# A four-layer graph network on one core: first matrix on two queues, the last mask turn one tile earlier, first weights and sigmoids around the end of a projection, one divisor product for the last tile

## The chip, the cores and the metric

The kernel runs on one core of a Trainium2 chip. The metric is the device time of one execution in microseconds, the median over several runs. The engines are named as in the profile: PE (matmul), DVE (vector), ACT (scalar), POOL (GpSimd) and SP (sync); PEld is PE's weight load, which overlaps its matmuls. SP, ACT and POOL can each issue DMAs.

## The reference, cut to what matters

A graph of 2708 nodes with 512 features passes four layers, each `x = layernorm(x + layer(x, adj))`. Layer 0 averages the first 64 neighbours of each node, layer 1 all of them, layer 2 is an eight-head graph attention, layer 3 an eight-head one followed by a one-head one and a two-layer MLP.

```python
# layer 0: mean of the first 64 neighbours, one matrix each for it and for x itself
keep = Ab & (jnp.cumsum(Ab.astype(jnp.int32), axis=1) <= neibor_num)
nb_mean = (keep @ X) / jnp.maximum(cnt, 1.0)
xj = leaky_relu(nb_mean @ W_nb.T + b_nb); xi = leaky_relu(X @ W_line.T + b_line)
# layer 1
agg = mask @ x / jnp.maximum(deg, 1.0)
out = relu(concat([x @ W_self + b_self, agg @ W_nb + b_nb]) @ W_comb + b_comb)
# layers 2 and 3, each head
Wh = einsum('ni,hio->hno', h, W)
e = leaky_relu(f1[:, :, None] + f2[:, None, :], 0.2)     # f1, f2 = Wh . a1, Wh . a2
attention = softmax(where(adj > 0, e, -9e15), axis=-1)
h_prime = einsum('hnm,hmo->hno', attention, Wh)
```

## The kernel before

The nodes are cut into NT = 22 tiles of 128 rows (the last, LAST, has 20). A scheduler orders each engine's instructions; where the kernel wants a fixed order it says so: `pe(...)` chains PE's instructions in program order, and `tc.issue_after(x)` holds what is issued inside it behind `x` on its engine. Each engine works through its own list in order.

**Layer 0, first loop (L291 to L339).** `transpose_weight` (L136) loads a 512x512 matrix in four pieces of 128 rows from SP, turns each on PE and copies it with DVE. Then, tile by tile: `keep_y` (product with the first matrix, split in a high part by ACT and a low one by DVE), the product with the second matrix, and beside them the adjacency: rows are loaded by POOL as bf16 (`load_mask`, L255), turned to 0/1 by an ACT sigmoid (`count`, L260), limited to the first 64 by DVE scans (`place`, L264), and turned on PE with ACT signs into `maskT` (`turn`, L273). 14 of the 22 row blocks are done there, at most one per tile; the loop at L320 turns a block one tile after it was placed. Its last pass, at the last tile, turns all. The remaining 8 row blocks are loaded from L353 on into `spare` and `w`; `spare` lies where the row blocks of the first loop were, so its first load waits for the last turn.

**Layer 0, second loop (L467).** PE multiplies `kT`, made from `maskT` by ACT (L350), with the high and low parts (L477), with the remaining row blocks' `count` (L262) between the `kT` of ACT.

**Projections (`project`, L587).** For each tile: transpose of the rows, product with all heads' weights into PSUM `pm` (L642), then `dcol` and `b` on DVE, `ecol` and `ucol` as exponentials on ACT (L663, L664), `vcol` (L677), `vrow` (L622, stored to DRAM by an ACT DMA), and `R2`, the scaled rows, on DVE (L671). The last tile stands twice in its key tile: on partitions 0 to 19 for even heads and 32 to 51 (from TWIN) for odd heads (L651 to L661, two halves `k`). After the last tile of a block of 11, DVE splits `ecol` and `ucol*ecol` into bf16 parts `parts_m`, `parts_c` (L680 to L689). The small copies of this split are L581 to L585.

**Attention (`heads_attention`, L755; `Weights`, L698).** 16 runs in all: two layers, each two blocks of columns (1408 and 1300) by four pairs of heads. In a run, for each of the 22 key tiles `j` (order L887: ten tiles, then LAST, then the rest) and each head: DVE makes the weights `e = max(v, u) * mask` (L718), ACT marks by a sigmoid where `v` is below `u` (`above`, L741, the tile `c`), and PE multiplies `e` with R2 into `po` (L910). For LAST there is one `e` and one `c` for both heads. `divisors` (L810) adds up, four key tiles at a time, the products of `c` with `parts_c`, for each head in four column groups (L814). Buffers: five `e`, eleven `c`; an `e` buffer is free when PE and ACT have read it. `vrow`'s PSUM comes free for `po` once ACT has read the last of it.

`Weights.first` (L730) lets a projection make four weight tiles ahead, from tile NT − 6 = 16 on, one per tile: `att.early` (two key tiles by two heads), held in order behind R2 of the tile before (L665). Their sigmoids are issued only in the attention (L907), where the scheduler is free to move them forward.

Of the kernel before, what the change touches and what calls it, by code (L numbers as in the profile page):

```python
# [13 lines left out]
AF = mybir.ActivationFunctionType  # L14
# [4 lines left out]
P = 128  # L19
D = 512  # L20
KD = D // P
EPS = 1e-5
ALPHA = 0.2
# [7 lines left out]
def kernel(  # L31
# [9 lines left out]
    nc = tc.nc  # L41
# [91 lines left out]
        nc.scalar.copy(dst[:, :, :n], ps[:, :, :n])  # L133
        return dst

    def transpose_weight(room, psum, dst, src):  # L136

        for ki in range(KD):
            wr = room[ki]
            nc.sync.dma_start(wr, src[ki * P:(ki + 1) * P, :])  # L140
            ps = psum.tile([P, KD, P], F32, name="ps_tr")
            for ko in range(KD):
                pe(nc.tensor.transpose(ps[:, ko, :], wr[:, ko * P:(ko + 1) * P], ident))
            nc.vector.tensor_copy(dst[:, :, ki * P:(ki + 1) * P], ps)
# [56 lines left out]
    with ExitStack() as phase:  # L201
# [89 lines left out]
        with ExitStack() as ph:  # L291
            st = ph.enter_context(tc.tile_pool(name="l0a", bufs=1))
            wnT, wlT = weight(), weight2
            room = [maskT[:, G + k, :4 * D].bitcast(F32) for k in range(2 * KD)]

            xs = rows_of(x)
            xTs = early(0, NT, lambda t, order=as_it_comes: transposed(ahead, ps_tr, xs(t), rows(t), "xT", order))

            transpose_weight(room[:KD], ps_tr, wnT, l0_w_nb)
            lows = {}
            for t in range(2):
                xT = xTs(t, order=pe)
                lows[t] = keep_y(t, P, product(xT, P, wnT, 0, pe))
            transpose_weight(room[KD:], ps_tr, wlT, l0_w_line)
            b_line = bias(bcast(l0_b_line, D))
            masks = early(1, HERE, lambda i: load_mask(i, st.tile([P, N], BF16, name="m", bufs=3)))
            masks(0)
            nc.gpsimd.memset(maskT[:, NT - 1, :], 0.0)  # L310
            nc.gpsimd.memset(maskT[:, :, N:], 0.0)
            counted = turned = 0
            for t in range(NT):
                n = rows(t)
                if t > 1:
                    lows[t] = keep_y(t, n, product(xTs(t, order=pe), n, wnT, 0, pe))
                xT = xTs(t)
                if t + 1 < NT:
                    xTs(t + 1, order=pe)
                while turned < counted - (t + 1 < NT):  # L320
                    for _ in turn(turned, masks(turned), lambda: sums(BF16, (P, G, P)), pe):
                        pass
                    turned += 1
                now = counted < min(HERE, -(-(t - 1) * HERE // (NT - 5)))
                if now:
                    m, places = masks(counted), st.tile([P, N // 2], BF16, name="places", bufs=1)
                    with tc.issue_after(highs[t].ins):
                        count(counted, m)
                    with tc.issue_after(lows[t].ins):
                        place(counted, m, places, 0, 2)  # L330
                pm = product(xT, n, wlT, 1, pe)
                u = sm.tile([P, D], F32, name="u")
                nc.vector.tensor_add(u[:n], pm[:n], b_line[:n])  # L333
                low = rows_made = leaky(u[:n], u[:n])
                nc.gpsimd.dma_start(r0_dram[t * P:t * P + n, :], u[:n])
                if now:
                    with tc.issue_after(low.ins):
                        place(counted, m, places, 1, 2)
                    counted += 1  # L339
# [238 lines left out]
    def split(pool, dst, src):  # L578

        rest = pool.tile([P, NT, H], F32, name="rest", bufs=1)[:, :src.shape[1], :src.shape[2]]  # L580
        nc.vector.tensor_copy(dst[:, :, :, 0], src)  # L581
        nc.vector.tensor_sub(rest, src, dst[:, :, :, 0])
        nc.vector.tensor_copy(dst[:, :, :, 1], rest)
        nc.vector.tensor_sub(rest, rest, dst[:, :, :, 1])
        nc.vector.tensor_copy(dst[:, :, :, 2], rest)  # L585

    def project(name, source, layer, v_dram, cuts, turned=None, first=None):  # L587
# [12 lines left out]
        with ExitStack() as ph:  # L600
# [16 lines left out]
            def keep_v(t):  # L617
                n = rows(t)
                vrow = sm.tile([heads, P], F32, name="vrow")
                ps = ps_v.tile([P, P], F32, name="ps_v")  # L620
                nc.tensor.transpose(ps[:heads, :n], bs[t][:n, :heads], ident[:n, :n])
                nc.scalar.activation(vrow[:, :n], ps[:heads, :n], AF.Exp, scale=ALPHA - 1.0)  # L622
                nc.scalar.dma_start(v_dram[:, t * P:t * P + n], vrow[:, :n])

            for t in range(NT):
# [55 lines left out]
                if t == z - 1:  # L681
                    if heads > 1:
                        ue = sm.tile([P, NT, H], F32, name="ue", bufs=1)[:, :z - a]
                        nc.vector.tensor_mul(ue, ucol[:, a:z], ecol[:, a:z])
                        split(sm, parts_m[:, a:z], ue)
                        for k in range(2):
                            nc.vector.tensor_scalar(pairs_c[:, a:z, :, k, 6 * k:6 * k + 3], parts_m[:, a:z, k::2, :],
                                                    -1.0, None, op0=OP.mult)
                            split(sm, pairs_c[:, a:z, :, k, 6 * k + 3:6 * k + 6], ecol[:, a:z, k::2])  # L689
            keep_v(NT - 1)  # L690
            sq = sm.tile([P, NT * H], F32, name="sq", bufs=1)[:, :NT * heads]
            dd = dcol[:, :, :heads]
# [5 lines left out]
    class Weights:  # L698


        def __init__(self, stack, name, blocks, v_dram):
            self.blocks, self.v_dram = blocks, v_dram
            self.W = max(self.width(b) for b in range(len(blocks)))
            self.pool = stack.enter_context(tc.tile_pool(name=f"{name}_att", bufs=2))

# [24 lines left out]
        def first(self, t):  # L730

            if t == NT - 8:
                self.vs = [self.load(0, h) for h in range(2)]
                self.early = []
            i = t - (NT - 6)
            if not 0 <= i < 4:
                return None
            self.early.append(self.weights(0, i % 2, i // 2, self.vs[i % 2]))
            return self.made
# [12 lines left out]
        oT_dram.append(dram.tile([D, (z - a) * P], F32, name=f"oT_dram{i}"))  # L752
        rc_dram.append(dram.tile([H, 12 * P], F32, name=f"rc_dram{i}"))

    def heads_attention(name, att, as_rows, meanwhile={}):  # L755

# [1 line left out]
        with ExitStack() as ph:  # L760
# [48 lines left out]

            def divisors(b, p, pair):  # L810
                for i, j, hs, cs in pair:
                    for h, c in zip(hs, cs):
                        for g, c0, c1 in groups(b):
                            pe(nc.tensor.matmul(p[32 * g:32 * g + 12, :c1 - c0], parts_c[:, j, h, :], c[:, c0:c1],  # L814
                                                start=(i == 0 and h == hs[0]), stop=(i == NT - 1 and h == hs[1])))
# [72 lines left out]
            for r, (b, h0) in enumerate(runs):  # L888
# [9 lines left out]
                for i_, j in enumerate(order):  # L898
                    if j == LAST:
                        es = [att.weights(b, h0, j, both)] * 2  # L900
                        cs = [att.above(b, h0, j, es[0])] * 2
                        if r + 1 < len(runs):
                            both = att.load_both(*runs[r + 1])
                    else:
                        es = ([att.weights(b, h, j, v) for h, v in zip(hs, vs)] if r or i_ > 1 else
                              att.early[2 * i_:2 * i_ + 2])
                        cs = [att.above(b, h, j, e) for h, e in zip(hs, es)]  # L907
                    for i, (c0, c1) in enumerate(parts):
                        for k, (h, e) in enumerate(zip(hs, es)):
                            pe(nc.tensor.matmul(po[i][HO * k:HO * k + HO, :c1 - c0], R2[:, j, h * HO:(h + 1) * HO],  # L910
                                                e[:, c0:c1], start=(i_ == 0), stop=(i_ == NT - 1)))
                    if len(pair) == 4:
                        divisors(b, pd[r % 2], pair)
                        pair = []
                    pair.append((i_, j, hs, cs))
                    for step in todo.get(i_, ()):
                        step()
# [206 lines left out]
    vd = [dram.tile([heads, N], F32, name=f"v_dram{i}") for i, heads in enumerate((H, H, 1))]  # L1124
    for i, source in enumerate((plain, summed)):
        with ExitStack() as ph:
            att = Weights(ph, f"a{2 + i}", blocks, vd[i])
            project(f"p{2 + i}", source, i, vd[i], blocks, first=att.first)
            heads_attention(f"a{2 + i}", att, i == 0, {
                9 + 4 * t: [lambda t=t: ready.update({t: elu_turned(None, t, t + 1)})] for t in range(3)} if i else {})  # L1130
    ph4 = fast.enter_context(ExitStack())
    att = Weights(ph4, "a4", quads, vd[2])
# [329 lines left out]
```

## Time and profile before

| | us |
|---|---|
| median of 3 runs | 2969.1 (2968.95 to 2974.76) |
| profiled execution | 2975.79 |
| its span | 2973.9 |
| PE / DVE / ACT busy in the span | 2879.2 / 1998.3 / 1536.7 |
| layer 0 first loop, second loop begins | 0 to 217.7 |
| projection of layer 2 / attention runs | about 880 to 975 / 975 to 1519 |
| projection of layer 3 / attention runs | about 1525 to 1626 / 1626 to 2173 |

"Busy" counts overlapping instructions of one engine once. A line of the timeline gives start, length, engine, line, operation, output and input, the number of instructions merged, and in brackets the idle time of that engine just before and what ended it. A busy PE is not a PE at its peak: its ends are modelled, and a stretched row of matmuls can hide short waits. Several groups run in parallel engines, so shares don't add up.

### The profile page before, as it was taken

To read this page: it belongs to the slowest core of one execution; us is meant where nothing else is said; L and a number is where in the kernel's file an instruction comes from. 1 tells how busy PE (TensorE), PEld (TensorE's weight loads), DVE (VectorE), ACT (ScalarE), POOL (GpSimd) and SP (SyncE) were. 2 spreads that over 40 slices of the span, in tenths; PEclk is the share of its full clock that TensorE was granted. 3 is DMA by queue.
4 is the path that set the end of the run, shared out by engine and by line. 5 is a ranking of instruction groups with operands and counts; after the bars stand their busy time and mean duration, and the time that the engine had idled before them with its cause. 6 is when DMAs were issued, how large, how long until landed. Compare 5 with 4: busy or idle time off the path is not lost. (4 is left out here: it accounts for less than half of the span.)

```text
span 2973.9 us, 36611 instructions
## 1 busy us (share of the span) xinstructions
PE 2879.2 (97%) x14462; PEld 1605.8 (54%) x14462; DVE 1998.3 (67%) x2406; ACT 1536.7 (52%) x1775; POOL 207.9 (7%) x344
## 2 busy tenths in 40 slices
PE   8999999999999999999999999999999999999998
PEld 3447766448888343444456334434475555555555
DVE  5966637543234899999977999999963535445342
ACT  3545533113224899999966899999951000000001
POOL 1110100101110000000012000000000000000001
PEclk9999999999999999999999999999999999999999
DMA  4532426322222011111144111121061000000000
GB/s 121 122 91 57 113 87 171 130 62 92 79 74 81 21 52 46 38 45 44 32 126 147 40 40 39 41 64 37 29 160 61 4 25 14 25 14 16 15 18 24
DMA packets 121153, 185.61 MB, mean 62 GB/s; under 512 B 41741, under 2 KB 66562, under 8 KB 120972
## 3 DMA queue, kind: packets, MB, share of 16 engines
q1 hardware_dynamic: 92096, 122.09, 13.7%
q0 software_dynamic: 18160, 57.39, 6.8%
q10 hardware_dynamic: 10716, 3.69, 0.5%
q8 instruction: 116, 1.90, 0.3%
q14 instruction: 65, 0.53, 0.1%
HBM read 153.10 MB, written 44.65 MB: 66 GB/s over the span
## 5 line engine op out<-in xcount | busy, mean ns | idle before, releaser
L718 DVE SCALAR_TENSOR_TENSOR e<-v_bc,ucol,maskT 128x1408 f32<-128x1408 f32 (+3 forms) x804 | 1135.3, 1467 | 328.0 <-PE pn L1091 315.0
L745 ACT ACTIVATE c<-e,bcol 128x1300 fp8e4<-128x1300 f32 (+1 forms) x688 | 968.3, 1423 | 77.4 <-DVE e L718 33.5
L910 PE MATMUL po<-e,R 128*64 128x512 f32 (+2 forms) x4224 | 905.9, 548 | 33.4 <-DVE e L718 25.9
L910 PEld LDWEIGHTS po<-e,R 128*64 128x64 f32 x4224 | 339.8, 137 | 566.4 <-issue 397.1
L1091 PE MATMUL pn<-e,R 128*128 128x512 f32 (+1 forms) x1056 | 413.4, 542 | 0.0
L1091 PEld LDWEIGHTS pn<-e,R 128*128 128x128 f32 x1056 | 191.1, 190 | 199.2 <-issue 196.1
L1042 ACT ACTIVATE w<-pl,b 128x256 f32<-128x256 f32 (+1 forms) x88 | 41.0, 466 | 373.1 <-PE pl L1040 365.2
L477 PE MATMUL acc<-yH,kT 128*128 128x512 f32 x484 | 198.1, 409 | 6.4 <-ACT kT L350 6.4
L477 PE MATMUL acc<-yL,kT 128*128 128x512 f32 x484 | 190.1, 393 | 0.0
L528 PE MATMUL acc<-yH,mf 128*128 128x512 f32 x484 | 188.4, 389 | 0.0
L528 PE MATMUL acc<-yL,mf 128*128 128x512 f32 x484 | 188.3, 389 | 0.0
L244 PE MATMUL pm<-w,xT 128*128 128x512 f32 (+1 forms) x376 | 172.9, 603 | 14.6 <-DVE yL L230 12.1
L642 PE MATMUL pm<-w,xT 128*128 128x264 f32 (+1 forms) x704 | 166.4, 389 | 5.5 <-DVE R L671 2.4
L244 PE MATMUL pm<-weight,xT 128*128 128x512 f32 (+1 forms) x344 | 158.3, 603 | 2.7 <-DVE u L333 1.9
L1040 PE MATMUL pl<-lin 128*128 128x256 f32 (+1 forms) x704 | 154.8, 374 | 2.8 <-DVE lin L939 2.8
L120 POOL TENSOR_TENSOR ln_rs<-ln_rs,half 128x1 f32<-128x1 f32 (+1 forms) x88 | 54.2, 616 | 1449.3 <-DVE ln_rs L119 1380.8
L1065 PE MATMUL pl<-lin,w 128*128 128x512 f32 x336 | 150.8, 593 | 0.0
L1040 PEld LDWEIGHTS pl<-lin 128*128 128x128 f32 x704 | 130.4, 192 | 33.7 <-issue 15.8
L525 ACT CAST mf<-maskT 128x1024 fp32r<-128x1024 fp8e4 (+1 forms) x66 | 64.5, 978 | 156.5 <-PE acc L528 152.9
L642 PEld LDWEIGHTS pm<-w,xT 128*128 128x128 f32 (+1 forms) x704 | 128.7, 188 | 30.2 <-ACT xT L133 4.5
L229 ACT CAST yH<-pm 128x512 fp32r<-128x512 f32 (+1 forms) x43 | 25.2, 586 | 225.1 <-PE pm L244 225.1
L350 ACT ACTIVATE kT<-maskT 128x512 fp32r<-128x512 fp8e4 (+1 forms) x132 | 77.5, 593 | 117.6 <-PE acc L477 117.5
(237 smaller groups left out, 2726.2 us busy)
## 6 DMA issues: line engine op xcount, KB each, us to landing
rows<-x_dram SPq DMA_DIRECT2D x63, 256.0 KB
v_bc<-v_dram SPq DMA_DIRECT2D x16, 704.0 KB
rows<-in_x_dram SPq DMA_DIRECT2D x42, 256.0 KB
x_dram<-u POOLq DMA_DIRECT2D x42, 256.0 KB, 2.3
v_bc<-v_dram SPq DMA_DIRECT2D x16, 650.0 KB
m<-in_adj_dram POOLq DMA_DIRECT2D x13, 677.0 KB, 7.0
r_dram<-u POOLq DMA_DIRECT2D x21, 256.0 KB, 2.3
rows<-r_dram SPq DMA_DIRECT2D x21, 256.0 KB
```

The source lines that it names most:

```text
L244: order(nc.tensor.matmul(pm[:n], xT[:, k, :n], w[:, k, :], start=(k == 0), stop=(k == KD - 1)))
L350: made = nc.scalar.activation(kT[:, :w], maskT[:, j, b[0] * P:b[0] * P + w], AF.Relu, scale=-1.0)
L477: nc.tensor.matmul(pa[t], kT[:, (t - b[0]) * P:(t - b[0] + 1) * P], y[:, j, :], start=(j == 0 and y is yH), stop=(j == NT - 1 and y is yL))
L525: nc.scalar.copy(mf[:, :g1 - g0, :], maskT[:, g0:g1, t * P:(t + 1) * P])
L528: nc.tensor.matmul(pa, mf[:, j - g0, :], y[:, j, :], start=(j == 0 and y is yH), stop=(j == NT - 1 and y is yL))
L642: nc.tensor.matmul(pm[a][:m, :D // 2 + heads], xT[:, k, :m], w[:, k, a, :D // 2 + heads], start=(k == 0), stop=(k == KD - 1))
L718: self.made = nc.vector.scalar_tensor_tensor(e[:, :w], v[:, :w], ucol[:, j, h:h + 1], maskT[:, j, c0:c0 + w], op0=OP.max, op1=OP.mult)
L745: nc.scalar.activation(c[:, :w], e[:, :w], AF.Sigmoid, bias=bcol[:, j, h:h + 1], scale=STEP, saturate=False)
L910: pe(nc.tensor.matmul(po[i][HO * k:HO * k + HO, :c1 - c0], R2[:, j, h * HO:(h + 1) * HO], e[:, c0:c1], start=(i_ == 0), stop=(i_ == NT - 1)))
L1040: nc.tensor.matmul(pl[:, :w], self.lin1[:, k, f * P:(f + 1) * P], h[:, k, :w], start=(k == 0), stop=(k == KD - 1))
L1065: nc.tensor.matmul(pl[:n], gT[:, f, (t - t0) * P:(t - t0) * P + n], self.lin2[:, f, :], start=(f == 0), stop=(f == KF - 1))
L1091: nc.tensor.matmul(pn[k][:, :w], R2[:, j, k * P:(k + 1) * P], e[:, :w], start=(j == 0), stop=(j == NT - 1))
```

## The change

Four edits.

1. `transpose_weight` takes a list of queues and deals the four pieces out in turn. The first matrix uses SP and ACT, the second still SP alone.
2. The loop at L320 stops holding a row block back at the last two tiles, not only at the last.
3. `Weights` gets `many`, the number of weight tiles made during the projection: five in layer 2, four in layer 3. In the attention's first run the weights come from `att.early` as long as there are any. The sigmoids of the first two key tiles are held behind `scaled["v"]`, the last `vrow` exponential of the projection.
4. For LAST the divisor product is made for the first head of the pair only. For it a copy is added at the end of the last block's split: in LAST's `parts_c` the even heads' columns 6 to 11 are filled from the odd heads', so that one product gives both (the two heads stand on different partitions).

```diff
-    def transpose_weight(room, psum, dst, src):
+    def transpose_weight(room, psum, dst, src, queues=(nc.sync,)):
         for ki in range(KD):
             wr = room[ki]
-            nc.sync.dma_start(wr, src[ki * P:(ki + 1) * P, :])
+            queues[ki % len(queues)].dma_start(wr, src[ki * P:(ki + 1) * P, :])
...
-            transpose_weight(room[:KD], ps_tr, wnT, l0_w_nb)
+            transpose_weight(room[:KD], ps_tr, wnT, l0_w_nb, (nc.sync, nc.scalar))
...
-                while turned < counted - (t + 1 < NT):
+                while turned < counted - (t + 2 < NT):
...
-                nc.scalar.activation(vrow[:, :n], ps[:heads, :n], AF.Exp, scale=ALPHA - 1.0)
+                scaled["v"] = nc.scalar.activation(vrow[:, :n], ps[:heads, :n], AF.Exp, scale=ALPHA - 1.0)
...
+                        if z == NT:
+                            nc.vector.tensor_copy(pairs_c[:, LAST, :, 0, 6:12], pairs_c[:, LAST, :, 1, 6:12])
...
-        def __init__(self, stack, name, blocks, v_dram):
-            self.blocks, self.v_dram = blocks, v_dram
+        def __init__(self, stack, name, blocks, v_dram, many=0):
+            self.blocks, self.v_dram, self.many = blocks, v_dram, many
...
-            if not 0 <= i < 4:
+            if not 0 <= i < self.many:
                 return None
...
-    def heads_attention(name, att, as_rows, meanwhile={}):
+    def heads_attention(name, att, as_rows, exps, meanwhile={}):
...
-                    for h, c in zip(hs, cs):
+                    for h, c in list(zip(hs, cs))[:1 if j == LAST else 2]:
...
-                        es = ([att.weights(b, h, j, v) for h, v in zip(hs, vs)] if r or i_ > 1 else
-                              att.early[2 * i_:2 * i_ + 2])
-                        cs = [att.above(b, h, j, e) for h, e in zip(hs, es)]
+                        es = [att.weights(b, h, j, v) if r or 2 * i_ + k >= att.many else att.early[2 * i_ + k]
+                              for k, (h, v) in enumerate(zip(hs, vs))]
+                        with tc.issue_after(exps.ins) if r == 0 and i_ < 2 else nullcontext():
+                            cs = [att.above(b, h, j, e) for h, e in zip(hs, es)]
...
-            att = Weights(ph, f"a{2 + i}", blocks, vd[i])
-            project(f"p{2 + i}", source, i, vd[i], blocks, first=att.first)
-            heads_attention(f"a{2 + i}", att, i == 0, {
+            att = Weights(ph, f"a{2 + i}", blocks, vd[i], 5 - i)
+            scaled = project(f"p{2 + i}", source, i, vd[i], blocks, first=att.first)
+            heads_attention(f"a{2 + i}", att, i == 0, scaled["v"], {
```

## The prediction

> **What bounds the kernel now.** I read the page's first two parts, then a table of stretches, the groups by form, and the timeline where the change acts.
>
> ```profile
> PE 2879.2 (97%) x14462; PEld 1605.8 (54%) x14462; DVE 1998.3 (67%) x2406; ACT 1536.7 (52%) x1775; POOL 207.9 (7%) x344
> PE   8999999999999999999999999999999999999998
> DVE  5966637543234899999977999999963535445342
> ```
>
> PE looks like the bound everywhere, but in the middle third DVE shows 9 as well. The table by stretch (us, then busy time of PE, PEld, DVE, ACT, POOL; clock; DMA) separates them; here are two of the sixteen runs of the two head-attention stages:
>
> ```profile
> 1046.00:1115.00 69.00, 67.92 (x463) 27.75 (x461) 68.47 (x49) 63.96 (x51) 0.00 (x0) 1.00 0.11 35
> 1322.00:1387.00 65.00, 63.89 (x457) 27.27 (x455) 65.00 (x51) 61.05 (x51) 0.00 (x0) 1.00 0.12 39
> ```
>
> DVE fills these runs. The groups by form confirm it:
>
> ```profile
> L718 DVE SCALAR_TENSOR_TENSOR e<-v_bc,ucol,maskT 128x1408 f32<-128x1408 f32 x336 | 542.1, 1677 | 10.1 <-PE po L910 5.0 <-DMA v_bc<-v_dram 4.1 <-ACT oT L920 0.9
> ```
>
> A weight tile `e` costs DVE 542.1/336 = 1.61 us. A run has 43 of them: 69.4 us, which is the run. PE's own work is less: twelve L910 instructions a key tile take 2.24 us where PE doesn't wait (48 in 8.95 us from 1287.10), 49 us a run, plus 11 rounds of 16 divisor products (7.7 us) and some turns: about 60 of 65 us. So in the attention stages a saving on PE is mostly slack, and time is won only by starting DVE's chain of `e` earlier. That chain starts at the end of each projection (layer 2, then layer 3):
>
> ```profile
> 965.97 1.28 ACT L745 ACT_TABLE_LOAD   x1
> 967.27 1.47 ACT L745 ACTIVATE c<-e,bcol 128x1408 fp8e4<-128x1408 f32 x1
> 968.75 1.28 ACT L622 ACT_TABLE_LOAD   x1
> 972.52 1.47 ACT L745 ACTIVATE c<-e,bcol 128x1408 fp8e4<-128x1408 f32 x1
> 974.01 1.28 ACT L655 ACT_TABLE_LOAD   x1
> 975.69 10.18 PE L910 MATMUL po<-e,R 128*64 128x512 f32 x38 [4.78 <-ACT vrow L622]
> 981.31 1.70 DVE L718 SCALAR_TENSOR_TENSOR e<-v_bc,ucol,maskT 128x1408 f32<-128x1408 f32 x1
> ...
> 1627.09 8.16 PE L910 MATMUL po<-e,R 128*64 128x512 f32 x38 [1.52 <-ACT vrow L622]
> 1629.70 3.28 DVE L718 SCALAR_TENSOR_TENSOR e<-v_bc,ucol,maskT 128x1408 f32<-128x1408 f32 x2 [2.52 <-PE po L910]
> ```
>
> Sigmoids and exponentials alternate on ACT with a table load at each turn; the last `vrow` stands behind them and holds PE back 4.78 us in layer 2, 1.52 in layer 3. DVE has five `e` ahead by then (five buffers) and goes on only when PE has read one.
>
> Two more places, at the end of layer 0's first loop and at the start:
>
> ```profile
> 214.92 0.73 POOL L257 DMA_DIRECT2D spare<-in_adj_dram  x1 [0.99 <-PE acc L280]
> 224.79 2.55 ACT L262 ACTIVATE spare<-spare,gate 128x2708 bf16<-128x2708 bf16 x1 [1.69 <-DMA spare<-in_adj_dram]
> 227.79 0.50 PE L477 MATMUL acc<-yH,kT 128*128 128x512 f32 x1 [3.37 <-ACT kT L350]
> 229.34 0.63 PE L477 MATMUL acc<-yL,kT 128*128 128x512 f32 x1
> ...
> 5.71 3.85 PE L143 MATMUL ps_tr<-ident,maskT 128*128 128x128 f32 x16 [5.71 <-DMA maskT<-in_L_gnn_W_nb_dram]
> 10.24 1.09 PE L131 MATMUL ps_tr<-ident,rows 128*128 128x128 f32 x4 [0.67 <-DMA rows<-in_x_dram]
> ```
>
> ACT waits 1.69 us for a mask row block that was asked for only after the last turn, and PE, starved of `kT`, waits 3.37 us. After it seven L477 start 0.43 us apart instead of 0.23 (the 0.63 us ones).
>
> **What the Trainium skill says.** "ScalarE: Activation LUTs", What ACT_TABLE_LOAD costs: about 1283 ns a load plus a drain of 1380 ns at each switch of set, and the rule to do all of one set first. The trace agrees on 1.28 us; it shows no drain beyond the sigmoid's own end (974.01 follows 972.52 + 1.47 at once). "TensorE: Matmul & The Clock Gate", Part 1: PE falls to half clock after some 3.4 us of idleness. The trace fits: 3.37 us idle, then half rate. "DMA: Bandwidth & Descriptors", Issuing engines are not separate DMA queues: a second issuer saves only issue time. No run shows this yet.
>
> **The change part by part**, against the profiled execution (2975.79 us, span 2973.9; the median of the three runs is 2969.1, so 6.7 lower).
>
> *First matrix on two queues.* SP issues two instead of four pieces before the `rows` loads, ACT the other two ahead of its bias load and first table load (idle until 11.36, so that costs nothing). The first piece keeps its place. PE's transposes then run 0.87 us a piece and wait for nothing but its arrival. Gain: the 0.67 us wait for `rows`, which now stand two issues (0.8 us) earlier. Loss: piece 1 shares the engines with piece 0; DMA share is 0.67 to 0.80 between 2 and 5 us, so not full. If the first landing slips by half of its 2 us of transfer, +1.0. I take −0.5 (−0.7 to +1.0).
>
> *Turn one tile earlier.* The instruction lists show the last turn (22 transposes, 1.34 us of PE) ahead of tile 20's second product instead of ahead of tile 21's; PE has no gap between 205 and 224, so its sum stays. DVE placed that mask by 193.7, so nothing waits. On POOL the load of `spare` moves before tile 20's store and `w`; it waits for the turn, so it goes out near 207.5 instead of 214.9 and, at its 9.9 us, lands by 218. ACT reaches L262 at 223.1: the 1.69 us go, what is late next is L262 itself (2.55 us), and PE still waits 1.68. If that is too short to drop the clock, 7 × 0.20 = 1.4 us go too. I take half of that: −2.4 (−1.7 to −3.1).
>
> *One divisor product.* It removes 4 matmuls in each of 16 runs. 32 of them take 1.41 us (1285.11 to 1286.52), so 4 take 0.18: 2.8 us of PE. The round in which they stand is followed by DVE-bound tiles, except in the two runs that also compute a block's mask products, where DVE waits for PE for 0.84 and 0.45 us. It adds a small copy on DVE per layer, 0.13 us between two `e` (as the split's copies cost there). I take −0.2 in sum without the copies, which I count below (−2.8 to 0).
>
> *First weights, and sigmoids after the exponentials.* Five planned `e` in layer 2, four in layer 3; five were ahead already in both (946.23 to 963.61), so the number matters little. The first five sigmoids now stand behind the last `vrow`. Layer 2: without table loads the projection keeps its 4.11 us a tile, so the last tile's products start at 945.40 + 5 × 4.11 = 965.95 instead of 966.84 and end at 969.7; `b`, two transposes, `vrow` (1.15 us) follow, PE starts at 970.9: 4.8 earlier. But the sixth `e` now waits for the first sigmoid as well, because that reads the buffer: 970.9 + 1.28 + 1.47 = 973.6. Behind it in DVE's queue stand the second half of R2's last tile and the split. ACT meanwhile loads exponentials, does three small ones, loads sigmoids, and ends the second sigmoid at 978.05. DVE: sixth `e` to 975.3, then 3.7 us of small steps (976.21 to 979.9 before), seventh `e` at 979.05, and then eight small steps lie between the next eight `e`, 0.13 each: the fifteenth starts at 979.05 + 8 × 1.73 = 992.9. Before, the eighth started at 984.76 and the fifteenth at 984.76 + 7 × 1.60 = 996.0. Gain 3.1.
>
> Layer 3 likewise: PE's wait for `xT` at 1608.89 (1.24 us) and one at 1621.72 (0.43) go, with some slip, so the last products start near 1619.8 instead of 1621.72, PE at 1624.6 (was 1627.09), first sigmoid done at 1627.4, sixth `e` 1627.5 (was 1629.70). But the small steps that lay between `e` before now stand in one block: seventh `e` at 1632.9, fifteenth at 1646.7; before, the fourteenth was at 1645.95, the fifteenth at 1647.66. Gain 1.0, or 1.4 by the nineteenth, where the old list still has small steps. Together −4.5. Bounds: −7.3 if PE's earlier starts (4.8 + 2.5) count in full, +2.8 if they don't come (1.7 and 1.1 more than what was gained). PE waits some 4 us for the eighth `e` and may drop its clock, 1.7 us; DVE is behind then, so this is hidden while PE has its 5 us of slack a run.
>
> Sum: −0.5 − 2.4 − 0.2 − 4.5 = −7.6. Profiled 2968.2; median **2961.5**.
>
> **The rivals.**
>
> 1. *The scalar queue takes the place of the table loads.* The start of DVE's chain gains nothing, since the first sigmoids, now late, hold the `e` buffers. For it: the sixth to tenth `e` wait for sigmoids that were done long before, and in layer 3 the margin is under 1 us (second sigmoid 1631.95, seventh `e` 1632.9). Against: a sigmoid takes 1.47, an `e` 1.61, so ACT catches up. The other parts remain: −3.1, 2966.
>
> 2. *PE is the bound after all.* For it: PE's 99% in part 2. Then the divisor products and PE's earlier starts count in full: −0.7 − 3.1 − 2.8 − 7.3 = −13.9, 2955. Against: the table by stretch.
>
> 3. *Slower.* The same sigmoids, but the projection does not end earlier, because PE's first L910 is held by something else than the table loads. Then each layer pays the load and the sigmoid ahead of the sixth `e`: +2.8. It decides from the point where PE's start gains less than 1.7 us in layer 2 and 1.1 in layer 3. With the first load at its bad end (+1.0) and the turn at −1.7: +2.1, 2971. To be 0.2% slower, PE would have to start 2 us later per layer. Against: the trace names `vrow` as the releaser in both layers.
>
> That the change doesn't do what it says is small: "two queues" may move nothing, worth 0.5.
>
> **How the numbers follow.** Forecast 0.60, first rival 0.22, second 0.08, third 0.10. The range leaves out the second rival and most of the third: 2956 to 2969. Runs of this kernel lie between 2968.95 and 2974.76, so I call 0.2%, 5.9 us, what can be told from no change: faster is below 2963.2. Of the forecast some 0.48 lies there, with the second rival 0.56; the rest of the forecast, the first and most of the third rival are the same, 0.37; slower 0.07.
>
> **What would show it.** Right: one table load pair at each projection's end, PE's first L910-type product near 971 (relative to a start that is some 3 us earlier), no wait of ACT on `spare`, runs still 69 and 65 us long. Wrong: DVE waiting for ACT before the seventh to tenth `e`, runs that get shorter by 0.18 us each (PE bound), a first transpose later than 5.7 us, or PE's first product waiting for something other than `vrow`.

## The result, and the profile after

The changed kernel takes 2960.8 us (median of 7 runs, 2958.79 to 2963.07), the kernel before 2971.67 (7 runs, the three of the table above among them, 2968.95 to 2974.76): a ratio of 0.9966, 95% interval 0.9956 to 0.9975. That is 10.9 us less by the medians, 10.1 by the ratio (7.4 to 13.1). The profiled executions differ by more, 2975.79 against 2960.23.

The page of the changed kernel has the same picture of busy shares:

```profile
PE 2872.9 (97%) x14398; PEld 1604.1 (54%) x14398; DVE 1998.5 (68%) x2408; ACT 1515.0 (51%) x1759; POOL 204.8 (7%) x344
```

PE has 64 instructions less (4 in each of 16 runs), DVE two more (the copies), and ACT 16 less and 22 us less: table loads between sigmoids and exponentials, of which there are 33 in the profile before and 17 here. Where the time went is read from the timeline, at the three places shown of the kernel before. Lines below L692 stand 3 further down after the change, those of the attention loop 5 (L718 is L721, L745 is L748, L910 is L915).

The start (timeline of the changed kernel, PE):

```profile
4.81 3.84 PE L143 MATMUL ps_tr<-ident,maskT 128*128 128x128 f32 x16 [4.81 <-DMA maskT<-in_L_gnn_W_nb_dram]
8.58 0.73 PE L131 MATMUL ps_tr<-ident,rows 128*128 128x128 f32 x4
9.98 3.70 PE L244 MATMUL pm<-w,xT 128*128 128x512 f32 x8 [0.68 <-ACT xT L133]
```

The first piece is there 0.90 us earlier (it was 5.71), the wait for `rows` is gone, and the first product starts 2.02 us earlier. Then something the change does not touch: this group of eight took 6.21 us before and takes 3.70 here, and another such group (5.40 at 27.23 before) takes 3.70 too. By the second tile's product with the second matrix the changed kernel is 6.23 us ahead.

The end of layer 0's first loop (timeline of the changed kernel; POOL, ACT and PE):

```profile
201.19 0.71 POOL L257 DMA_DIRECT2D spare<-in_adj_dram  x1 [3.49 <-PE acc L280]
...
216.46 2.54 ACT L262 ACTIVATE spare<-spare,gate 128x2708 bf16<-128x2708 bf16 x1
...
219.45 0.50 PE L477 MATMUL acc<-yH,kT 128*128 128x512 f32 x1 [1.56 <-ACT kT L350]
219.79 0.39 PE L477 MATMUL acc<-yL,kT 128*128 128x512 f32 x1
```

`spare` goes out at 201.19 instead of 214.92 (7.2 us earlier, apart from the lead of 6.6 that the kernel has by then), ACT no longer waits for it, PE waits 1.56 us instead of 3.37, and no 0.63 us products follow. The lead over the kernel before grows from 6.56 us (first L477) to 8.34 and, after the products that ran slowly before, to 9.71.

The ends of the two projections (timeline of the changed kernel; ACT, PE and DVE of layer 2, then PE and DVE of layer 3):

```profile
961.78 1.28 ACT L748 ACT_TABLE_LOAD   x1
963.08 1.47 ACT L748 ACTIVATE c<-e,bcol 128x1408 fp8e4<-128x1408 f32 x1
964.56 1.28 ACT L655 ACT_TABLE_LOAD   x1
...
966.16 1.28 ACT L748 ACT_TABLE_LOAD   x1
...
961.69 7.35 PE L915 MATMUL po<-e,R 128*64 128x512 f32 x36 [0.86 <-ACT vrow L622]
...
964.72 1.68 DVE L721 SCALAR_TENSOR_TENSOR e<-v_bc,ucol,maskT 128x1408 f32<-128x1408 f32 x1 [2.79 <-ACT c L748]
970.13 1.67 DVE L721 SCALAR_TENSOR_TENSOR e<-v_bc,ucol,maskT 128x1408 f32<-128x1408 f32 x1
...
1612.24 7.31 PE L915 MATMUL po<-e,R 128*64 128x512 f32 x36 [0.86 <-ACT vrow L622]
...
1615.01 1.68 DVE L721 SCALAR_TENSOR_TENSOR e<-v_bc,ucol,maskT 128x1408 f32<-128x1408 f32 x1 [2.52 <-ACT c L748]
```

PE's wait for the last `vrow` falls from 4.78 to 0.86 us, and from 1.52 to 0.86. DVE now waits for the first sigmoid, and between its sixth and seventh weight tile lies the block of small steps. The lead is 8.95 us at the projection's tile 16 and 12.10 at the fifteenth weight tile; in layer 3 it grows from 12.28 (tile 16) to 13.53 at the fifteenth weight tile and 14.11 at the end of the first run.

### The profile page after: what moved, and what is told of

It reads as the page before. It is cut to its first block, busy times and chain, and to the rows that moved or that the text cites. A ratio compares the mean times of both kernels' runs of the same rounds, so it can differ in the third digit from the quotient of the medians.

```text
span 2958.4 us, 36480 instructions
## 1 busy us (share of the span) xinstructions
PE 2872.9 (97%) x14398; PEld 1604.1 (54%) x14398; DVE 1998.5 (68%) x2408; ACT 1515.0 (51%) x1759; POOL 204.8 (7%) x344
## 5 line engine op out<-in xcount | busy, mean ns | idle before, releaser
L721 DVE SCALAR_TENSOR_TENSOR e<-v_bc,ucol,maskT 128x1408 f32<-128x1408 f32 (+3 forms) x804 | 1135.2, 1465 | 329.2 <-PE pn L1096 315.3
L748 ACT ACTIVATE c<-e,bcol 128x1300 fp8e4<-128x1300 f32 (+1 forms) x688 | 965.8, 1422 | 65.4 <-DVE e L721 20.8
L915 PE MATMUL po<-e,R 128*64 128x512 f32 (+2 forms) x4224 | 907.7, 549 | 31.2 <-DVE e L721 27.9
L915 PEld LDWEIGHTS po<-e,R 128*64 128x64 f32 x4224 | 342.7, 137 | 563.2 <-issue 388.3
L477 PE MATMUL acc<-yH,kT 128*128 128x512 f32 x484 | 197.3, 408 | 4.6 <-ACT kT L350 4.6
L477 PE MATMUL acc<-yL,kT 128*128 128x512 f32 x484 | 189.2, 391 | 0.0
L244 PE MATMUL pm<-w,xT 128*128 128x512 f32 (+1 forms) x376 | 170.4, 596 | 14.3 <-DVE yL L230 12.1
L244 PE MATMUL pm<-weight,xT 128*128 128x512 f32 (+1 forms) x344 | 156.7, 598 | 2.7 <-DVE u L333 1.9
```

What stands on the lines that cost most here:

```text
L244: order(nc.tensor.matmul(pm[:n], xT[:, k, :n], w[:, k, :], start=(k == 0), stop=(k == KD - 1)))
L477: nc.tensor.matmul(pa[t], kT[:, (t - b[0]) * P:(t - b[0] + 1) * P], y[:, j, :], start=(j == 0 and y is yH), stop=(j == NT - 1 and y is yL))
L721: self.made = nc.vector.scalar_tensor_tensor(e[:, :w], v[:, :w], ucol[:, j, h:h + 1], maskT[:, j, c0:c0 + w], op0=OP.max, op1=OP.mult)
L748: nc.scalar.activation(c[:, :w], e[:, :w], AF.Sigmoid, bias=bcol[:, j, h:h + 1], scale=STEP, saturate=False)
```

## The experiments

Times are medians; a ratio is to the kernel before on the same chip: 2971.91 us for the first four, 2972.43 for the next four, 2970.71 for the last four. The medians of one kernel move by one or two microseconds from one set of runs to the next, so each part is also read by its place: how far an experiment's timeline is ahead of the profile shown of the kernel before, at one instruction and at a later one.

**1. First matrix alone.** The kernel before with this edit only (shown without the new argument of `transpose_weight`):

```diff
-            transpose_weight(room[:KD], ps_tr, wnT, l0_w_nb)
+            transpose_weight(room[:KD], ps_tr, wnT, l0_w_nb, (nc.sync, nc.scalar))
```

> The kernel before with only the first matrix on two queues. Theory: the transfer gains 0.9 us at the first landing and 0.7 us of the wait for rows, and no more; that the profile of the whole change stood 6.2 us ahead by its 27th microsecond, 4.6 of it from multiplications at full instead of half clock, was chance, since the clock falls at no fixed point. So a median 1.6 us shorter (1 to 2.2). Rival: the half clock at the start of the kernel before was caused by its wait for rows, and goes with it; then 4 to 6.2 us shorter, and in the profile every L244 group of eight below 30 us takes 3.7 us. Rival as on record: the first piece does not land earlier, 0.5 us shorter.

Measured: 2969.35 us (13 runs), ratio 0.9991 (0.9983 to 0.9999), 2.6 us less. First transpose 4.61, first product 9.92 (2.08 earlier), and no half clock at the start; yet its median has not gained the 6.3 us by which its profile is ahead at the 27th microsecond.

**2. Turn alone.**

```diff
-                while turned < counted - (t + 1 < NT):
+                while turned < counted - (t + 2 < NT):
```

> The kernel before with only the turn one tile earlier. Theory: the ACT wait for spare goes (1.69 us) and PE's wait before the L477 after it falls below 2 us, which keeps the clock: 3.1 us shorter (2.4 to 3.4), no L477 group of 0.63 us each after it. Rival: the half clock there comes by chance, then 1.7 us shorter and the slow group may still be seen.

Measured: 2967.17 us (13 runs), ratio 0.9991 (0.9983 to 0.9999). By place: 0.16 us behind at the first L477, 1.62 ahead after the wait (1.57 us long), 3.15 ahead 16 products later. So 1.8 us by the wait and 1.5 by the clock.

**3. Divisor alone.** Edit 4, shown without its copy.

```diff
-                    for h, c in zip(hs, cs):
+                    for h, c in list(zip(hs, cs))[:1 if j == LAST else 2]:
```

> The kernel before with only the one divisor product at the last tile and the copy of the divisor parts for it. Theory: PE's saving of 0.18 us a run lies in slack, -0.2 +0.26 for the two copies: no change, -0.7 to +0.3 us. Rival: PE is the bound of the runs, then 2.8 us shorter and each run of 43 weight tiles 0.18 us shorter.

Measured: 2967.91 us (13 runs), ratio 0.9989 (0.9980 to 0.9999): 4.0 us less by medians, 3.3 by the ratio, with an interval that reaches from 0.3 to 5.9. That is no slack of 0.2. Yet the runs are not 0.18 us shorter each either: those of 65.5 us stay at 65.5.

This profile also answers the question of the clock, since its start is the kernel before's. Its timeline there and at the L477 after ACT's wait (PE):

```profile
11.67 3.70 PE L244 MATMUL pm<-w,xT 128*128 128x512 f32 x8 [0.67 <-ACT xT L133]
...
222.97 0.50 PE L477 MATMUL acc<-yH,kT 128*128 128x512 f32 x1 [3.05 <-ACT kT L350]
223.30 0.40 PE L477 MATMUL acc<-yL,kT 128*128 128x512 f32 x1
```

Full clock at the start with one queue, and full clock after a wait of 3.05 us: neither slow stretch belongs to the code alone. Over all profiles, the wait for `kT` is 2.90 to 3.56 us in the seven without the turn edit, and the clock fell in four of them; in the seven with it the wait is 1.53 to 1.57 us, and the clock fell in none.

**4. First weights and sigmoids alone.** Edit 3 of the change.

> The kernel before with only the five (layer 2) and four (layer 3) first weights and the first sigmoids behind the last vrow. Theory, from the profile of the whole change: 3.2 us in layer 2 and 1.5 to 2.3 us in layer 3, so 4.7 to 5.5 us shorter. Forecast on record: 4.5 (3.1 and 1.4). Rival: the DVE chain starts no earlier because the sigmoids hold its buffers: 0 to 1 us shorter. Rival: PE's earlier start counts in full: 5.05 and 2.6, together 7.6 us shorter.

Measured: 2968.93 us (13 runs), ratio 0.9991 (0.9981 to 1.0002). By place: the lead grows from 0.17 us before the projection of layer 2 to 3.35 at the fifteenth weight tile, and from 3.96 at the last run of layer 2 to 5.69 at the first of layer 3: 3.2 and 1.7 us. The median gives 3.0, below the 4.9 of the places; the interval of the ratio (0.6 us longer to 5.6 shorter) holds both, and no gain as well.

**5 to 8. All again, two with a part left out, and one with an addition.** Experiment 6 takes the divisor edit and its copy out, experiment 7 the second queue. Experiment 8 holds the sigmoids behind the twin's last exponential instead of the last `vrow`:

```diff
-                            nc.scalar.activation(ucol[at, t, i::2], d2, AF.Exp, scale=1.0 - ALPHA)
+                            scaled["v2"] = nc.scalar.activation(ucol[at, t, i::2], d2, AF.Exp, scale=1.0 - ALPHA)
...
-            heads_attention(f"a{2 + i}", att, i == 0, scaled["v"], {
+            heads_attention(f"a{2 + i}", att, i == 0, scaled["v2"], {
```

> The changed kernel once more, so that the next three are read beside it on one chip. By the places in the profiles so far the four parts are worth 2.0 (first matrix), 3.2 (turn), 0.5 to 1 (divisor) and 4.9 us (sigmoids): 10.6 to 11.1 us shorter than the kernel before. Adding the medians of the four parts alone gives 14.3 us; if the parts alone were read without error the whole would be 14 us shorter.

> The changed kernel with both divisor products at the last tile again, and no copy. Theory from the lengths of the runs in the profiles: 0.3 to 1.2 us longer than the changed kernel. Rival, from the median of the divisor part alone: 3.5 us longer. Rival as on record, PE as the bound: 2.8 us longer.

> The changed kernel with the first matrix on one queue again. Theory: first landing near 6.0 us instead of 4.8, first L244 2 us later, 2.0 us longer by the median; whether L244 below 30 us runs at half clock differs from profile to profile and does not depend on the queues. Rival: the half clock comes with the one queue, then 4 to 6 us longer.

> The changed kernel with the first sigmoids behind the last small exponential (the twin's, L657) instead of the last vrow. ACT then loads its table once at the end of a projection instead of three times, and DVE has the splits of the divisor parts in the 2.5 to 2.8 us in which it waits for the first sigmoid in the changed kernel. Theory: the fifteenth weight tile starts 2.4 us earlier in each of the two layers, 4.8 us shorter than the changed kernel, about 2956.0. Rival: the first sigmoid itself sets the pace, and the second to fifth sigmoids hold the buffers: 0 to 1 us a layer. Rival: the small steps still stand between the weight tiles, no gain.

| | median us (5 runs each) | ratio to before |
|---|---|---|
| 5, the change | 2959.37 | 0.9959 (0.9945 to 0.9973) |
| 6, without divisor | 2962.34 | 0.9964 (0.9950 to 0.9977) |
| 7, without two queues | 2959.69 | 0.9960 (0.9946 to 0.9973) |
| 8, exponentials first | 2955.17 | 0.9941 (0.9928 to 0.9955) |

The four parts alone add up to 14.3 us by medians and 11.3 by ratios; the whole gives 13.1 and 12.2 here, 10.9 and 10.1 at first. With the intervals of the parts, each 2.4 to 3.1 us either way, this is no contradiction. Leaving the divisor out costs 3.0 us by medians and 1.5 by the ratios, leaving the queue out 0.3; with five runs each, neither is clear of noise. With one queue again the first product starts at 11.62 instead of 10.17, as expected, but by the first L477 the two profiles are equal (213.11 and 213.06): here it was the kernel with two queues that lost 1.7 us to a slow stretch at 23.4. One and a half microseconds at the start are smaller than that draw.

Experiment 8 is the fastest version: its slowest run (2957.25 us) is below the fastest of experiment 5 (2958.34). Its timeline at the end of layer 2's projection (ACT, then DVE):

```profile
961.22 1.28 ACT L748 ACT_TABLE_LOAD   x1
962.52 22.12 ACT L748 ACTIVATE c<-e,bcol 128x1408 fp8e4<-128x1408 f32 x16
...
964.02 1.69 DVE L721 SCALAR_TENSOR_TENSOR e<-v_bc,ucol,maskT 128x1408 f32<-128x1408 f32 x1
965.62 0.24 DVE L585 CAST parts_m<-rest 128x88 bf16<-128x88 f32 x1
965.74 1.68 DVE L721 SCALAR_TENSOR_TENSOR e<-v_bc,ucol,maskT 128x1408 f32<-128x1408 f32 x1
```

One table load instead of three, and sixteen sigmoids in a row. The sixth weight tile starts at the end of the first sigmoid as before, but the small steps have been done in the wait, so the seventh follows 1.72 us later instead of 5.41. By place, counted from tile 16 of each projection to the fifteenth weight tile, it gains 2.9 us over the changed kernel in layer 2 and 2.7 in layer 3; by medians 4.2 in all, by the ratios 5.3. Expected were 2.4 a layer, 4.8 in all.

**9. Zero products.** What the divisor part takes away, doubled and added to the kernel before (`none` is a tile of zeros):

```diff
+                            if j == LAST:
+                                pe(nc.tensor.matmul(p[32 * g:32 * g + 12, :c1 - c0], none, c[:, c0:c1],
+                                                    start=False, stop=False))
```

> The kernel before with two more divisor-shaped products a run and column group at the last tile, with a block of zeros as weights, so the result is unchanged: 8 matmuls more in each of 16 runs, twice what the change takes away. If PE has slack there, as the prediction held (0.2 us for 4 matmuls a run), 0 to 0.5 us longer. From the lengths of the runs with and without the divisor part (1.1 us less with it): about 2.2 us longer, in the wide runs one to three of each layer. If the medians of the divisor part hold (2.2 to 3.5 us): 4.4 to 7 us longer. If PE is the bound: 16 x 0.35 = 5.6 us longer, 0.35 in every run.

Measured: 2975.32 us (21 runs), ratio 1.0013 (1.0006 to 1.0021): 3.9 us longer by the ratio (1.8 to 6.2), 4.6 by medians, for 5.6 us of PE. So PE's work in the runs is not free. The waits of DVE's `e` in the second to eighth run of layer 2 say how (waits of the kernel before, of the changed kernel, and of this one; total, times, longest):

```profile
DVE e L718 <- DMA v_bc<-v_dram: 2.8, 4, 1.0
DVE e L718 <- PE po L910: 2.5, 3, 1.2
```

```profile
DVE e L721 <- DMA v_bc<-v_dram: 2.4, 3, 0.9
DVE e L721 <- PE po L915: 1.1, 2, 0.7
DVE e L721 <- ACT oT L925: 1.0, 1, 1.0
```

```profile
DVE e L720 <- DMA v_bc<-v_dram: 4.9, 4, 2.5
DVE e L720 <- PE po L915: 1.6, 2, 1.2
```

At the change of a run, and in the run with the mask products, DVE does wait for PE. With two divisor products (the kernel before, experiments 1 and 6) the waits for PE are 2.5 us in each profile, with one (the changed kernel, experiments 3 and 5) 1.1. A part is given back at once: where PE held `e` for 1.23 us at the start of a run, the changed kernel waits 0.99 us for ACT's `oT`. All waits of `e` together are 5.1 to 5.4 us in the first three profiles, 4.1 to 4.7 in the other three, and 6.5 with the zero products, one of them 2.5 us for a `v_bc` that came later. In layer 3 they are 3.3 to 4.2 us in all seven profiles, with no order among them.

The length of these seven runs, from the first weight tile of the second to the end of the last weight tile of the eighth, can be read in every profile. In layer 2 it is 473.7 to 474.7 us in the seven profiles with two products (mean 474.2), 473.1 to 473.7 in the six with one (473.5), and 477.4 with the zero products; in layer 3 the means are 473.8 and 473.3, and 473.8 with the zero products. So of the 3.9 us for the added products 3.2 are found in layer 2 (0.5 of them small steps of DVE that fall in there), and the products taken away are worth 0.7 us in layer 2 and 0.5 in layer 3 (where the profiles of the two kinds overlap), 1.2 in all. The timed comparisons of the divisor part (1.5 to 4.0 us) suggest more, but their intervals reach down to 0.3 us and less; whether more is there stays open.

**10. First weights only.** The changed kernel without `issue_after` on the sigmoids.

> The changed kernel with five and four first weights but the first sigmoids free to go as soon as their weights are there. Theory: the gain is in the order on ACT, so the table loads come back ahead of the last vrow; PE's first po product comes again 2.5 to 5 us later, and the kernel is 4 to 5.5 us longer than the changed one (2964 to 2966). Rival: the five planned weights are what counts; no more than 1 us longer.

Measured: 2964.89 us (20 runs), ratio 0.9980 (0.9973 to 0.9987), 4.1 to 5.5 us longer than the changed kernel's two medians (other sets of runs; by the ratios 4.2 and 6.2). Its ACT and PE at the end of layer 2's projection (timeline):

```profile
962.86 1.28 ACT L748 ACT_TABLE_LOAD   x1
964.15 1.47 ACT L748 ACTIVATE c<-e,bcol 128x1408 fp8e4<-128x1408 f32 x1
965.64 1.28 ACT L655 ACT_TABLE_LOAD   x1
...
967.32 8.24 PE L915 MATMUL po<-e,R 128*64 128x512 f32 x26 [4.77 <-ACT vrow L622]
```

A sigmoid is back ahead of the last `vrow` (967.11), with a table load on either side, the profile has 33 table loads again, and PE waits 4.77 us as it did before. The gain is the order on ACT. The number of first weights is worth nothing that shows: the 5.8 us by which this kernel is still ahead of the kernel before are about what the places give the other three parts (5.7 to 6.2).

**11 and 12. The bias, one run each.** Experiment 11 keeps one queue but moves the bias load, first on ACT's queue in the kernel before, behind the first tiles' copies; experiment 12 has two queues with the bias still first on ACT's. The edit of experiment 11, and the bias load as it stands in the timeline of the kernel before (ACT):

```diff
-            b_line = bias(bcast(l0_b_line, D))
+            with tc.issue_after(highs[0].ins):
+                b_line = bias(bcast(l0_b_line, D))
```

```profile
0.73 0.42 ACTq L223 DMA_DIRECT2D bias<-in_L_gnn_b_line_dram  x1
```

> The kernel before with the load of the bias (256 KB, first on ACT's queue) behind the first tile's copies, all four pieces of the matrix still on SP. If the first piece landed 1.2 us earlier in the changed kernel because the bias no longer shares the engines with it: first transpose near 4.8 us. If it is the second queue: near 6.0 us, as in the kernel before.

> The kernel before with the first matrix on two queues, but the bias ahead of its two pieces on ACT's queue. If the second queue is what brings the landing forward: first transpose near 4.8 us. If it is that the bias went behind the matrix: near 6.0 us, and a wait for piece 1 after the first four transposes.

Measured (timeline of experiment 11, then of experiment 12, PE):

```profile
3.92 1.94 PE L143 MATMUL ps_tr<-ident,maskT 128*128 128x128 f32 x8 [3.92 <-DMA maskT<-in_L_gnn_W_nb_dram]
6.91 1.09 PE L143 MATMUL ps_tr<-ident,maskT 128*128 128x128 f32 x4 [1.05 <-DMA maskT<-in_L_gnn_W_nb_dram]
9.48 1.08 PE L143 MATMUL ps_tr<-ident,maskT 128*128 128x128 f32 x4 [1.48 <-DMA maskT<-in_L_gnn_W_nb_dram]
11.64 1.09 PE L131 MATMUL ps_tr<-ident,rows 128*128 128x128 f32 x4 [1.07 <-DMA rows<-in_x_dram]
```

```profile
5.93 1.09 PE L143 MATMUL ps_tr<-ident,maskT 128*128 128x128 f32 x4 [5.93 <-DMA maskT<-in_L_gnn_W_nb_dram]
```

Without the bias ahead the first piece lands at 3.92, with two queues but the bias first at 5.93, no earlier than with one queue (5.7 to 6.3 in six profiles). So it is the bias going behind the matrix that brings the first landing forward, which the edit does in passing. It does not suffice: in experiment 11 the later pieces and `rows` come late and the rows' transposes start at 11.64; in experiment 12 they start at 10.73; only with both, at 8.4 to 8.7. Experiment 11 changes one more thing: the second matrix's loads go out at 4.04 us instead of 5.76, ahead of the first matrix's last pieces, so how much of their lateness is due to these loads and how much to the one queue is not shown.

## Why the prediction was right, and where not

The time (2961.5 forecast, 2960.8 measured) and the direction are right. But two errors cancelled, and that the time came within 0.7 us is luck. The gain was 10.9 us, not 7.6 (7.6 is at the edge of the interval, 7.4 to 13.1; the second set gave 13.1 by medians); and the median the 7.6 were taken from, 2969.1 of three runs, lay low: larger sets of the same kernel gave 2970.7 to 2972.4.

- **The first weights and sigmoids: right, within 0.3 us.** Shifted by the lead on arrival (8.95 us), the forecast for layer 2 reads: PE 961.95, sixth tile 964.65, seventh 970.10, fifteenth 983.95. Measured: 961.69, 964.72, 970.13, 983.84. In layer 3, shifted by 12.28: 1612.32, 1615.22, 1620.62, 1634.42; measured 1612.24, 1615.01, 1620.40, 1634.13. The gain is 3.15 and 1.25 us at the fifteenth tile (forecast 3.1 and 1.0), and 1.8 in layer 3 by the end of the first run (forecast 1.4 by the nineteenth tile). Experiment 10 shows the cause: with the order on ACT given back, the gain goes. The first rival, ACT holding the chain up between the seventh and the tenth tile, did not come: after the seventh the tiles follow at 1.67 to 1.75 us.
- **The turn: right mechanism, the uncertain half came in.** The load of `spare` moved as said, ACT's wait went, PE kept 1.56 us (forecast 1.68). "I take half of that" of the 1.4 us of clock: in the profiles compared it came in full, 3.15 us in all, just beyond the range of 1.7 to 3.1. But without this edit the clock fell in four of seven profiles only, so half was about right on average and the full sum a draw. The Trainium skill's figure ("TensorE: Matmul & The Clock Gate", Part 1: some 3.4 us of idleness) is no sharp bound here: a wait of 2.96 us (experiment 1) was followed by half clock, one of 3.05 was not.
- **The first matrix: the failed step is "The first piece keeps its place".** It landed 0.90 us earlier, and the first product 2.02; over six profiles without and six with the edit (experiments 11 and 12 aside) the first product starts at 11.9 and 10.1 on average. The prediction noted that the two pieces go "ahead of its bias load" and priced it at nothing, though 256 KB in the way of the first piece, issued at 0.73 us, were in the trace. The loss that it feared from piece 1 is there, if experiment 11's one run is typical: 3.92 us without the second queue, 4.6 to 4.9 with it, and the move of the bias outweighs it. "DMA: Bandwidth & Descriptors", Issuing engines are not separate DMA queues, agrees with this: a second queue alone (experiment 12) brought the first landing no gain. The timed worth of this edit, 0.3 to 2.6 us, is not settled better than that. By the first L477 the same six profiles with the edit are 3.5 us ahead on average (211.1 to 213.3 against 213.1 to 217.9), twice what they were at the first product, since groups of L244 at half clock are fewer: three before 30 us, against seven without. Whether the edit makes them rarer or six profiles happened to draw so is not shown.
- **One divisor product: the failed step is "mostly slack".** Where −0.2 was taken, the lengths of the runs say 1.2, the waits of `e` in layer 2 alone 0.8, and the timed comparisons 1.5 to 4.0. The prediction had seen the two waits for PE of 0.84 and 0.45 us (both in one run of layer 2) and missed a third, 1.23 at the change of a run; of these the changed kernel keeps 0.68 and 0.45, and 0.99 for ACT in place of the third. The second rival, PE as the bound, is right at these places and wrong for the narrow runs of 65.5 us, which did not get shorter. Adding is not the mirror of taking away: of twice as much PE work, added in experiment 9, 3.9 of 5.6 us come out (1.8 to 6.2), of the 2.8 us taken away some 1.2 by place.
- **The third rival** needed PE's first product to be held by something else than the table loads. It was not: counted from tile 16, it starts 5.05 and 2.57 us earlier (forecast 4.8 and 2.5).

## What to carry to other kernels

When two kinds of function alternate on one engine with a table load at each turn, look for what the switch stands ahead of and give the order by hand; and put all of one kind first, the last small one too, since the wait that remains is then free for small work (experiment 8). Before pricing a saving as slack, list the bounding engine's own waits over the whole stage and see whom they name: three short waits of DVE for PE in one layer, 2.5 us in sum, were enough here to make PE's work count in part. A gain read from one pair of profiles holds the draw of the clock in it: compare several profiles at one place before giving it to the change.

## What was not expected of the hardware

Apart from the end of the program, the half clock comes in the fourteen profiles in stretches of 3.41 us or twice that, mostly at the same few places of the program (near 27, 220 to 229, 970, 1515 to 1535, 1625 and 2850 to 2870 us); near 970 in thirteen of the profiles, at each of the others in some only. The times at which full clock was first granted at the start were 8.8 us in the changed kernel, 9.7 and 13.9 in experiments 5 and 6 with the same two queues, and 17.1 and 9.9 in the kernel before and experiment 3 with one. Together with a stretch near 27 that makes up to 4.5 us between two executions of the same start: experiment 3 was that much ahead of the kernel before at the 33rd microsecond, with no edit before it. It makes up most of the difference between 15.5 us by the profiles and 10.9 by the medians.
